# Moving half of a conversion to VectorE and counting four groups in a row, in a two-layer graph kernel

## The chip, the cores and the metric

The kernel runs on one core of a Trainium2 chip. The metric is the device time of one execution in microseconds (us); the median of three runs stands for a kernel. Before the change it is 272.93 us (272.83 to 273.19).

## The reference

Two graph layers over 4096 nodes with 64 features and a dense 4096x4096 adjacency of zeros and ones (about 16 ones in a row).

```python
# layer 0: each row weighs its last 100 neighbours by powers of 1/2, by rank within the row
support = x @ W0
rank = cumsum(adj != 0, axis=1); deg = rank[:, -1:]; k = minimum(deg, 100)
pos = rank - (deg - k)
w = mask * where(pos > 0, 0.5 ** (k - pos), 0)
x = layernorm(x + w @ support + b0)
# layer 1: mean over the neighbours, linear, relu, row norm
h = (adj @ x + x) / (sum(adj, 1) + 1)
out = relu(concat([x, h]) @ W1 + b1)
x = layernorm(x + out / maximum(norm(out), 1e-12))
```

## The kernel before

The transposed adjacency is cut into 8 **slabs** g of 512 target rows, and each slab into 8 **groups** k of 512 source rows, k running from 7 down to 0. A group (g, k) is a tile `a` of 128x4x512 in bf16, 512 KB in SBUF, cast from f32 by the DMA that loads it. Every group is loaded once. The 64 groups in the order (0,7), (0,6) ... (0,0), (1,7) ... (7,0) are numbered j = 0 to 63 here, and the main loop takes one group in each **step** i = 0 to 63, so step i works on group j = i, and slab g takes the steps 8g to 8g+7.

One step puts these pieces on TensorE, in this order: the **counts** of groups of the next chunk (`count`, line 233: how many ones each column has, four matmuls a group), **weigh** (line 261: eight half-size matmuls at line 270 and four at line 280, whose result in PSUM is the exponent of the weight; ScalarE turns one half of it into `w` at line 287, VectorE the other at line 288), up to four matmuls of the **second** layer (`some_sums`, line 344, matmul at line 307), **spread** (line 252, one matmul `rep`, and ScalarE's `near` at line 257), and **gather** of the step before (line 293, four matmuls at line 298). Then follow the hooks of the layer-0 epilogue: pz in step 8g+9, px in 8g+13, pu in 8g+14, and their parts on ScalarE, VectorE and GpSimd.

A **chunk** is a run of groups of one slab that share one `near`. Chunks are of one group in slab 0, two in slabs 1 to 3, four in slabs 4 to 7 (line 92). While a chunk is worked on, the groups of the next one are counted: `shares` (line 511) deals them out over its steps and joins two at a time, so that a chunk of two counts the two next groups in its first step, and a chunk of four counts two in its first and two in its third step. A chunk's count ends in an eviction `cs` by VectorE (line 247, or 249 for the first of a slab), which `spread` reads. TensorE, VectorE and ScalarE each run their instructions in this written order.

**Loads and buffers.** `load_next` (line 100) issues the loads on GpSimd's queue; six go out ahead of the loop, and step i issues load i+6. The bf16 tiles have 23 buffers (line 77). So load 23 and every later one needs a buffer that an earlier group has given back, and buffers are handed out in the order in which they come free. A group gives its buffer back in one of three ways:

- groups k = 7 to 4 of slabs 0 to 3 are copied to fp8 by `keep_next` (line 313), a half group (128x1024) in each of the steps 8 to 39, on ScalarE (line 320); the buffer is free after the second half;
- groups listed in `jobs` (line 325) give it back once the second layer has used them (line 307). The list is worked off in its order, one group a step, and a group k may be used from step 8(k+1)+6 on (`ready`, line 332), when x1hl, the layer-0 result of slab k, is there. Its first entries are (0,0), (0,1), (1,0), (1,1), (2,0), (2,1), (3,0), its last (6,0), (6,1), (6,2);
- the others stay to the end.

GpSimd's queue also carries the loads of x (`load_x`, step 8g+3) and the sums `add_b0` (step 8g+7). It runs in order: a load that waits for its buffer holds back everything behind it.

After step 63 the rest of the second layer runs, with the epilogue of layer 1.

Of the kernel before, what the change touches and what calls it, by code (L numbers as in the profile page):

```python
# [40 lines left out]
def adj_resnorm_kernel(  # L41
# [26 lines left out]
    nc = tc.nc  # L68
    D = w0.shape[0]
    NG, NK = adjT.shape[0], adjT.shape[1]  # L70
# [18 lines left out]

    chunks = []  # L90
    for g in range(NG):
        n = 1 if g == 0 else 2 if g < 4 else 4
        chunks += [[(g, k) for k in range(k0, k0 - n, -1)] for k0 in range(NK - 1, -1, -n)]
    steps = [s for c in chunks for s in c]
    when = {s: i for i, s in enumerate(steps)}

    A = [[None] * NK for _ in range(NG)]
    loads = iter(steps)

    def load_next(n=1, pieces=1):  # L100
        for _ in range(n):
            s = next(loads, None)
            if s is None:
                return
            g, k = s
            a = a16p.tile([P, KB, R], BF16, tag="a16", name=f"a16_{g}_{k}")
            for h in range(pieces):
                qs = slice(h * KB // pieces, (h + 1) * KB // pieces)
                nc.gpsimd.dma_start(out=a[:, qs, :], in_=adjT[g, k][:, qs, :])  # L109
            A[g][k] = a  # L110
# [8 lines left out]
    def load_xp(k):  # L119
        nc.gpsimd.dma_start(out=xp[:, ts(k, KB), :], in_=x_pairs[:, ts(k, KB), :])  # L120
# [112 lines left out]
    def count(g, k, first, last):  # L233
        if first:
            cnt[g] = ps_m.tile([P, R], F32, tag="m", name=f"cnt_{g}_{k}")
        for q in range(KB):
            nc.tensor.matmul(  # L237
                cnt[g][q * 32 : (q + 1) * 32, :],
                lhsT=pick[:, PW - 2 * k : PW - 2 * k + 32],
                rhs=A[g][k][:, q, :],  # L240
                start=first,
                stop=last,
            )
        if last:
            new = one.tile([P, R], BF16, tag="cs", name=f"cs_{g}_{k}")
            if g in cs:
                nc.vector.tensor_tensor(new, cnt[g], cs[g], ALU.add)  # L247
            else:
                nc.vector.tensor_copy(new, cnt[g])
            cs[g] = new  # L250

    def spread(g, k):

        pr = ps_m.tile([P, R], F32, tag="m", name=f"rep_{g}_{k}")
        nc.tensor.matmul(pr, lhsT=further, rhs=cs[g], start=True, stop=True)  # L255
        near[g] = epi.tile([P, R], BF16, tag="near", name=f"near_{g}_{k}")
        nc.scalar.activation(near[g], pr, AF.Relu, bias=most, scale=-1.0)  # L257
# [3 lines left out]
    def weigh(g, k, nr):  # L261

        w = wp.tile([P, KB, R], I16, tag="w", name=f"w_{g}_{k}")
        v = [ps_v.tile([P, 2, R], F32, tag="v", name=f"v_{g}_{k}_{i}") for i in range(2)]
        for i in range(2):
            for r in range(2):
                for c in range(2):
                    nc.tensor.matmul(  # L270
                        v[i][halves[c], r, :],
                        lhsT=tri[halves[r], :],
                        rhs=A[g][k][halves[r], 2 * i + c, :],
                        start=True,
                        stop=False,
                    )
        for i in range(2):
            for r in range(2):
                rows = slice((2 * i + r) * 32, (2 * i + r + 1) * 32)
                nc.tensor.matmul(  # L280
                    v[i][:, r, :],
                    lhsT=mine[rows, 2 * k : 2 * k + 2, :],
                    rhs=nr[rows, :],
                    start=False,
                    stop=True,
                )
        nc.scalar.activation(w[:, 0:2, :], v[0], AF.Relu, bias=less)  # L287
        nc.vector.tensor_scalar(w[:, 2:4, :], v[1], -STEP * MAX_NEIGH, 0.0, ALU.add, ALU.max)  # L288
        return w
# [3 lines left out]
    def gather(g, k, w):  # L293
        if k == NK - 1:
            acc0[g] = ps_a.tile([P, R], F32, tag="acc0", name=f"acc0_{g}")
        for q in range(KB):
            b = k * KB + q
            nc.tensor.matmul(  # L298
                acc0[g],
                lhsT=xhl[:, b, :],  # L300
                rhs=w[:, q, :].bitcast(BF16),
                start=(k, q) == (NK - 1, 0),
                stop=(k, q) == (0, KB - 1),
            )
# [5 lines left out]
    to_keep = [(g, k, h) for g in range(KEPT) for k in range(NK - 1, KEPT - 1, -1) for h in range(2)]  # L310
    kept = {}

    def keep_next():
        if not to_keep:
            return
        g, k, h = to_keep.pop(0)
        if h == 0:
            kept[g, k] = a8p.tile([P, KB, R], F8, tag="a8", name=f"a8_{g}_{k}")
        qs = slice(h * KB // 2, (h + 1) * KB // 2)
        nc.scalar.copy(kept[g, k][:, qs, :], A[g][k][:, qs, :], saturate=False)  # L320
        if h == 1:
            A[g][k] = kept[g, k]

# [7 lines left out]

    def ready(i, g, b):
        k = b // KB
        return i >= NK * (k + 1) + 6 and i >= when[g, k]

    def evict_part(g):
        acc = acc1.pop(g)
        if g in part:
            nc.vector.tensor_tensor(part[g], acc, part[g], ALU.add)
        else:  # L340
            part[g] = const.tile([P, R], F32, name=f"part_{g}")
            nc.vector.tensor_copy(part[g], acc)

    def some_sums(i, n):

        done = None
        while n and todo and done is None and ready(i, todo[0][0], todo[0][1]):
            g, b, first, last = todo.pop(0)
            if first:
                acc1[g] = ps_a.tile([P, R], F32, tag="acc1", name=f"acc_part_{g}_{b}")  # L350
            second(acc1[g], g, b, first, last)
            have[g] = b // KB + 1
            n -= 1
            if last:
                done = g
        return done
# [104 lines left out]
    def run(i, engine):  # L461
        for fn, args in hooks.pop((i, engine), []):
            fn(*args)

    for k in range(NK):
        i = when[0, k]
# [7 lines left out]
    for g in range(NG - 1):  # L474
        i = NK * (g + 1)
# [32 lines left out]
    for c, chunk in enumerate(chunks):  # L508
        ahead = chunks[c + 1] if c + 1 < len(chunks) else []
        n, m = len(chunk), len(ahead)  # L510
        shares = [ahead[i * m // n : (i + 1) * m // n] for i in range(n)]
        for i in range(0, n - 1, 2):

            shares[i : i + 2] = [shares[i] + shares[i + 1], []]
        nr = near[chunk[0][0]]
        for (g, k), share in zip(chunk, shares):
            i = when[g, k]
            run(i, ACT)
            run(i, POOL)
            load_next()  # L520
            if i < 3:
                load_xp(2 - i)

            w = weigh(g, k, nr) if i == 0 else None
            for s in share:
                count(*s, s == ahead[0], s == ahead[-1])
            w = w or weigh(g, k, nr)
            run(i, "ACT, late")
            done = some_sums(i, QUOTA)
            if share and share[-1] == ahead[-1]:  # L530
                spread(*ahead[-1])
            if i >= NK:
                keep_next()
            if held is not None:
                gather(*held)
            held = (g, k, w)
            run(i, PE)
            run(i, DVE)
            if done is not None:
                evict_part(done)  # L540
# [278 lines left out]
```

## Time and profile before

| | |
|---|---|
| median of 3 runs | 272.93 us |
| the profiled execution | 273.33 us |
| its span, first to last instruction | 271.5 us |
| TensorE busy in the span | 87% |
| VectorE, ScalarE, GpSimd busy | 65%, 58%, 23% |
| mean granted TensorE clock | 0.965 |
| loads of the adjacency | 65 DMAs, 9.7 us median to landing |
| conversions to fp8 on ScalarE | 32 of 1.04 us |
| counts evicted (`cs`), spreads (`rep`, `near`) | 28 each |

The profile comes from one execution. Its page shows busy shares by engine and by fortieth of the span; the timeline lists every instruction of an engine with its start, its length, and what ended the idle time before it; another answer gives the time from a DMA's issue to its landing. A matmul's length there is from start to modelled end, so matmuls in a row overlap: the distance from one start to the next is what a piece costs. Where a step's work begins is seen from its group of eight matmuls `v<-a,tri` of line 270: step 7 begins at 35.39 us, step 16 at 64.88, step 24 at 89.47, step 32 at 114.59, step 56 at 191.94.

### The profile page before, as it was taken

What the parts mean: (1) busy time and instruction counts of PE and PEld (TensorE: products, weight loads), DVE (VectorE), ACT (ScalarE), POOL (GpSimd) and SP (SyncE); (2) the same over time, 40 slices, a digit from 0 to 9 for tenths busy, and PEclk for the clock granted to TensorE, in tenths of its full rate; (3) what the DMA queues carried; (4) which work ended last, traced back from release to release, by engine and by line L of the source; (5) the groups of instructions that cost most, each with busy time, mean ns of one, the idle gap of its engine ahead of it and who ended that gap; (6) DMA issues with size and microseconds to landing.
All of it is one profiled execution on the core that took longest, in us unless ns stands there. A gap on an engine that the chain in (4) does not pass through costs nothing.

```text
span 271.5 us, 4838 instructions
## 1 busy us (share of the span) xinstructions
PE 237.3 (87%) x1865; PEld 105.0 (39%) x1865; DVE 176.3 (65%) x480; ACT 157.9 (58%) x226; POOL 61.9 (23%) x111
## 2 busy tenths in 40 slices
PE   8397688979899999999899999999998999997820
PEld 2122124334434343443344344434343546555710
DVE  5566634875596778367846684576577456597884
ACT  4456627897798869768854463436545322146351
POOL 8565551231101320322122121210200000221100
PEclk9979959999999999999999999999999999999985
DMA  6999999999997999799999999990500000010010
GB/s 97 195 230 234 241 212 214 222 214 214 223 214 141 165 211 214 124 171 214 182 179 205 203 162 180 168 168 12 98 2 0 0 2 0 0 42 20 19 58 21
DMA packets 12072, 37.13 MB, mean 137 GB/s; under 512 B 2066, under 2 KB 3218, under 8 KB 12050
## 3 DMA queue, kind: packets, MB, share of 16 engines
q0 software_dynamic: 10128, 35.66, 68.1%
q1 hardware_dynamic: 1922, 1.18, 1.5%
q8 instruction: 14, 0.23, 0.3%
q14 instruction: 8, 0.07, 0.1%
HBM read 69.34 MB, written 1.05 MB: 259 GB/s over the span
## 4 chain that ended last, share of the span: by engine, by line
PE 51%; DVE 11%; ACT 8%; issue 3%; POOL 1%; DVEq 0%; POOLq 0%; ACTq 0%
PE acc L298 10%; PE acc_part L307 9%; PE v L270 8%; PE v L280 5%; ACT w L287 4%; PE acc_right L307 3%; DVE w L288 3%; PE cnt L237 3%; PE vb L307 3%; PE pu L447 2%; PE va L307 2%; PE pz L594 2%; PE pz L395 2%; DVE x L422 1%; ACT a L320 1%
## 5 line engine op out<-in xcount | busy, mean ns | idle before, releaser
L288 DVE TENSOR_SCALAR w<-v 128x1024 int16<-128x1024 f32 x64 | 78.2, 1222 | 45.3 <-PE v L280 45.2
L287 ACT ACTIVATE w<-v,less 128x1024 int16<-128x1024 f32 x64 | 71.3, 1114 | 56.9 <-PE v L280 39.9
L298 PE MATMUL acc<-w,xhl 128*128 128x512 bf16 x256 | 67.2, 385 | 2.4 <-ACT hT L389 2.1
L109 POOL DMA_DIRECT2D a<-in_adjT_dram x65 | 35.5, 548 | 122.1 <-PE acc_part L307 49.9
L270 PE MATMUL v<-a,tri 64*64 64x512 bf16 x512 | 42.0, 397 | 4.3 <-ACT w L287 2.6
L298 PEld LDWEIGHTS <-xhl 128*128 128x128 f16 x256 | 23.9, 99 | 32.5 <-issue 9.5
L320 ACT CAST a<-a 128x1024 fp8e4<-128x1024 bf16 x32 | 33.3, 1039 | 0.0
L307 PEld LDWEIGHTS <-x1hl 128*128 128x128 f16 x224 | 19.8, 98 | 27.0 <-issue 5.7
L307 PE MATMUL acc_part<-a,x1hl 128*128 128x512 bf16 x108 | 28.0, 381 | 1.8 <-ACT x1hl L434 1.3
L247 DVE TENSOR_TENSOR cs<-cnt,cs 128x512 bf16<-128x512 f32 x20 | 13.8, 691 | 20.5 <-PE cnt L237 20.4
L237 PE MATMUL cnt<-a,pick 128*32 128x512 bf16 x256 | 21.9, 399 | 6.0 <-DMA a<-in_adjT_dram 6.0
L280 PE MATMUL v<-near,mine 32*128 32x512 bf16 x256 | 25.7, 391 | 0.2 <-ACT near L257 0.2
L270 PEld LDWEIGHTS <-tri 64*64 64x64 bf16 x512 | 12.6, 106 | 30.2 <-issue 28.0
L257 ACT ACTIVATE near<-rep,most 128x512 bf16<-128x512 f32 x28 | 19.1, 682 | 3.8 <-PE rep L255 3.7
L633 POOL TENSOR_TENSOR y<-y,x 128x256 f32<-128x256 f32 x7 | 5.0, 726 | 56.1 <-DVE y L630 56.1
L280 PEld LDWEIGHTS <-mine 32*128 32x128 bf16 x256 | 6.5, 91 | 24.9 <-issue 24.9
L255 PE MATMUL rep<-cs,further 128*128 128x512 bf16 x28 | 11.2, 400 | 3.7 <-DVE cs L247 1.7
L307 PE MATMUL acc_right<-a,x1hl 128*128 128x512 fp8e4 (+1 forms) x56 | 12.7, 379 | 0.0
L237 PEld LDWEIGHTS <-pick 128*32 128x32 bf16 x256 | 4.6, 94 | 19.8 <-issue 11.5
L655 ACT ACTIVATE o<-y,off,r_l 128x64 f32<-128x64 f32 x28 | 9.7, 428 | 3.1 <-issue 1.7
L382 DVE BATCH_NORM_STATS2 st_l<-y 128x6 f32<-128x64 f32 x60 | 9.0, 214 | 0.7 <-POOL y L633 0.6
L427 ACT CAST x1hl<-x 128x256 f16<-128x256 f32 x8 | 3.2, 406 | 10.1 <-DVE x L422 10.1
(139 smaller groups left out, 238.6 us busy)
## 6 DMA issues: line engine op xcount, KB each, us to landing
a<-in_adjT_dram POOLq DMA_DIRECT2D x63, 512.0 KB, 9.7
c<-in_x_pairs_dram POOLq DMA_DIRECT2D x8, 128.0 KB, 11.6
x<-in_x_dram POOLq DMA_DIRECT2D x8, 128.0 KB, 7.9
out_dram<-o SPq DMA_DIRECT2D x7, 128.0 KB, 1.7
a<-in_adjT_dram POOLq DMA_DIRECT2D x2, 256.0 KB, 4.7
out_dram<-o_7a SPq DMA_DIRECT2D x1, 64.0 KB, 1.9
out_dram<-o_7b SPq DMA_DIRECT2D x1, 64.0 KB, 1.5
w_sb<-in_L_gnn_weight_dram SPq DMA_DIRECT2D x2, 16.0 KB, 6.5
```

Source lines behind the costliest of these rows:

```text
L109: nc.gpsimd.dma_start(out=a[:, qs, :], in_=adjT[g, k][:, qs, :])
L237: nc.tensor.matmul(cnt[g][q * 32 : (q + 1) * 32, :], lhsT=pick[:, PW - 2 * k : PW - 2 * k + 32], rhs=A[g][k][:, q, :], start=first, stop=last,
L247: nc.vector.tensor_tensor(new, cnt[g], cs[g], ALU.add)
L255: nc.tensor.matmul(pr, lhsT=further, rhs=cs[g], start=True, stop=True)
L257: nc.scalar.activation(near[g], pr, AF.Relu, bias=most, scale=-1.0)
L270: nc.tensor.matmul(v[i][halves[c], r, :], lhsT=tri[halves[r], :], rhs=A[g][k][halves[r], 2 * i + c, :], start=True, stop=False,)
L280: nc.tensor.matmul(v[i][:, r, :], lhsT=mine[rows, 2 * k : 2 * k + 2, :], rhs=nr[rows, :], start=False, stop=True,)
L287: nc.scalar.activation(w[:, 0:2, :], v[0], AF.Relu, bias=less)
L288: nc.vector.tensor_scalar(w[:, 2:4, :], v[1], -STEP * MAX_NEIGH, 0.0, ALU.add, ALU.max)
L298: nc.tensor.matmul(acc0[g], lhsT=xhl[:, b, :], rhs=w[:, q, :].bitcast(BF16), start=(k, q) == (NK - 1, 0), stop=(k, q) == (0, KB - 1),)
L307: nc.tensor.matmul(acc, lhsT=x1hl[:, b, :], rhs=A[g][b // KB][:, b % KB, :], start=first, stop=last)
L320: nc.scalar.copy(kept[g, k][:, qs, :], A[g][k][:, qs, :], saturate=False)
```

## The change

Four edits.

1. **Chunks** (line 92): one group in slabs 0 and 1, two in slab 2, four in slabs 3 to 7.
2. **Shares**: where the next chunk has more than one group, all of it is counted in the first step of the present chunk. So a chunk of four counts its four next groups in a row in its first step.
3. **Conversion**: the half groups of the odd steps go to VectorE as a `tensor_copy` (the same 128x1024 from bf16 to fp8), those of the even steps stay on ScalarE. Each group so has one half on each engine, and its buffer is free after VectorE's.
4. **Loads and readiness**: the steps 16, 17 and 18 issue two loads each, so that step i from 18 on issues load i+9 in place of i+6; and the second layer may use a group from step 8(k+1)+7 on in place of +6.

```diff
     for g in range(NG):
-        n = 1 if g == 0 else 2 if g < 4 else 4
+        n = 1 if g < 2 else 2 if g < 3 else 4
         chunks += [[(g, k) for k in range(k0, k0 - n, -1)] for k0 in range(NK - 1, -1, -n)]
...
-    def keep_next():
+    def keep_next(i):
...
-        nc.scalar.copy(kept[g, k][:, qs, :], A[g][k][:, qs, :], saturate=False)
+        if i % 2:
+            nc.vector.tensor_copy(kept[g, k][:, qs, :], A[g][k][:, qs, :], saturate=False)
+        else:
+            nc.scalar.copy(kept[g, k][:, qs, :], A[g][k][:, qs, :], saturate=False)
...
     def ready(i, g, b):
         k = b // KB
-        return i >= NK * (k + 1) + 6 and i >= when[g, k]
+        return i >= NK * (k + 1) + 7 and i >= when[g, k]
...
         shares = [ahead[i * m // n : (i + 1) * m // n] for i in range(n)]
-        for i in range(0, n - 1, 2):
-            shares[i : i + 2] = [shares[i] + shares[i + 1], []]
+        if m > 1:
+            shares = [ahead] + [[]] * (n - 1)
...
-            load_next()
+            load_next(2 if 2 * NK <= i < 2 * NK + 3 else 1)
...
             if i >= NK:
-                keep_next()
+                keep_next(i)
```

## The prediction

> **What bounds the kernel now.** I read the page first: TensorE is busy 87% of the span, and the chain that ended last is mostly TensorE. Then the fortieths, where the loads show:
>
> ```profile
> PEclk9979959999999999999999999999999999999985
> DMA  6999999999997999799999999990500000010010
> ```
>
> The DMA engines are full until about 81 us (the 13th digit is the first 7 after the start) and the clock dips twice, the second time at 34 to 41 us. Then TensorE's timeline by steps. Steps 7, 24 and 55 to 56, each line a start, a length and the idle time before it:
>
> ```profile
> 34.84 0.62 PE L237 MATMUL cnt<-a,pick 128*32 128x512 bf16 x4 [2.68 <-DMA a<-in_adjT_dram]
> ...
> 89.47 0.63 PE L270 MATMUL v<-a,tri 64*64 64x512 bf16 x8
> 90.03 0.39 PE L280 MATMUL v<-near,mine 32*128 32x512 bf16 x4
> 90.35 1.04 PE L307 MATMUL acc_part<-a,x1hl 128*128 128x512 bf16 x4
> 91.22 0.38 PE L255 MATMUL rep<-cs,further 128*128 128x512 bf16 x1
> 91.44 1.03 PE L298 MATMUL acc<-w,xhl 128*128 128x512 bf16 x4
> ...
> 188.68 0.63 PE L270 MATMUL v<-a,tri 64*64 64x512 bf16 x8
> 189.24 0.39 PE L280 MATMUL v<-near,mine 32*128 32x512 bf16 x4
> 189.57 1.04 PE L307 MATMUL acc_part<-a,x1hl 128*128 128x512 bf16 x4
> 190.44 1.03 PE L298 MATMUL acc<-w,xhl 128*128 128x512 bf16 x4
> 191.40 0.62 PE L237 MATMUL cnt<-a,pick 128*32 128x512 bf16 x8
> 191.94 0.63 PE L270 MATMUL v<-a,tri 64*64 64x512 bf16 x8
> ```
>
> Step 24 has no gap: each piece starts where the one before ends. Start to start, weigh costs 0.56 + 0.33, second 0.87, rep 0.22, gather 0.96 (0.86 before a hook); elsewhere in the timeline a counted group costs 0.28, pz 1.01, px 0.53, pu 0.99. Until step 8 the loads bound the kernel (`cnt` waits seven times for them, 6.0 us in all, 2.68 the longest), from step 24 on TensorE's own work.
>
> Third, GpSimd's timeline, for loads that wait for a buffer:
>
> ```profile
> 83.19 0.53 POOL L109 DMA_DIRECT2D a<-in_adjT_dram  x1 [5.03 <-ACT a L320]
> 84.60 0.53 POOL L109 DMA_DIRECT2D a<-in_adjT_dram  x1 [0.88 <-PE rep L255]
> ...
> 190.90 0.53 POOL L109 DMA_DIRECT2D a<-in_adjT_dram  x1 [11.30 <-PE acc_part L307]
> ```
>
> These are loads 30, 31 and 63. Load 63 takes the buffer of (6,0), used last by the `acc_part` at 189.57. It is issued 2.22 us after its step's start and lands 5.0 later; so does load 30, issued into an idle queue. That is the least that any load after the first shows. With the queue full loads land 2.45 us apart: the times to landing of loads 13 to 27 put 13 at 44.6, 19 at 59.7, 23 at 69.6, 27 at 79.8.
>
> Last the clock, by stretches (length; TensorE, its loads, VectorE, ScalarE, GpSimd; clock; DMA share; GB/s):
>
> ```profile
> 24.00:28.00 4.00, 2.77 (x24) 0.91 (x23) 2.42 (x4) 2.40 (x4) 2.08 (x4) 1.00 1.06 242
> 30.60:34.00 3.40, 1.26 (x8) 0.31 (x7) 1.60 (x5) 1.86 (x3) 1.80 (x4) 1.00 1.07 224
> 34.00:40.80 6.80, 5.96 (x37) 1.40 (x36) 2.55 (x4) 1.69 (x2) 3.66 (x7) 0.50 1.06 213
> 40.80:44.20 3.40, 2.84 (x29) 1.03 (x22) 1.93 (x3) 2.61 (x4) 0.53 (x1) 1.00 1.07 214
> ```
>
> After 3.4 us at 37% busy the clock is halved for 6.8; stretches at 69% keep it.
>
> **What the Trainium skill says.** "TensorE: Matmul & The Clock Gate", Part 1: a free-running window of about 3.4 us, the clock halved after an idle one and restored after a busy one. The rows above agree: halved stretches of 3.4 (13.5 to 16.9) and 6.8 us. "VectorE: DVE Perf Modes", the perf-mode tier table: a copy in SBUF runs at four, two or one elements a cycle, by type and place; no such fp8 copy is in the trace. "SBUF: State Buffer", two separate sides: a VectorE copy in a two-port mode locks GpSimd out, which writes the load descriptors. The trace doesn't isolate it.
>
> **The change part by part.**
>
> *Conversion.* ScalarE loses 16 x 1.04 = 16.6 us. VectorE's price: row L214 turns 256 f32 into f16 in SBUF in 0.28 us; a four times larger copy at the same two a cycle is some 0.7 (estimate: 0.28 us + 768 elements two a cycle of the same page's 0.96 GHz, 0.40 us). Both ends, by the skill's modes: 0.4 and 1.2. So 16 x 0.7 = 11 us on an engine that is 65% busy, on odd steps, where it waits 2 us or more for TensorE in most (2.03 before `w` at 115.69). I take nothing; if the cover is gone, at 1.2, up to 0.5 a step in steps 13, 21, 29, 37.
>
> *Chunks.* Slab 1 spreads four times more and slab 3 twice less: two more `rep` (0.22), `cs` (0.69), `near` (0.68). In slab 1 the loads hide it.
>
> *Steps 7 to 22: gain, then lost to the loads.* Step 7 counts one group, not two, so the 2.68 us and the dip behind it go. Singles then follow the landings, and by adding pieces I get step 16 at about 60.1, against 64.88. But step 22 now counts loads 24 to 27 at once. Load 27 lands at 79.4 (79.8 less some 0.4, since the x load now stands behind it); the DMA has been full from the start, so nothing earlier in the kernel moves it. TensorE is there at about 75.5. Its weigh starts at 79.7 (before: 81.64): 1.9 us are left.
>
> *Step 24: a new wait.* It counts 28 to 31 in one go, at the head of the step. By the order of instructions load 31, group (3,0), takes the buffer of (0,1), which the second layer gives back in step 23, one step later than before. Step 23 starts at 79.7 + 0.56 + 0.33 + 0.22 + 0.86 + 0.99 = 82.7, load 31 is issued at +2.2 and lands at +5.0: 89.9; with the last 0.28 and some issue, step 24 starts at 90.3, against 89.47. Before, 31 was counted in step 30. Behind the waiting count stand all of TensorE's work, VectorE's `cs` and, after it, `w`. So the gain up to here is -1.9 + 2.7 = +0.8. The extra loads of steps 16 to 18 do nothing here: buffers and DMA decide.
>
> *Steps 24 to 55.* Work before: 31 steps x 1.85, less 12 x 0.1, hooks 10.1, 32 groups counted 8.8, 10 rep 2.2, 21 second 18.3: 95.6 of the 99.2 us, so 3.6 us of waits. After: 28 groups, 8 rep, 22 second (one was delayed): 94.8. Of the waits, 0.93 (rep on ScalarE's x1T at 109.26) and 0.52 (second on x1hl at 133.71) go with the new counts and readiness, 0.32 (on `part`) probably; I leave 1.9 for steps without second, where `w` sets the pace. 96.7, that is -2.5 (bounds -0.8 and -4.4). The other counts of four have their last load 0.1 to 3 us early by the same sum (steps 28, 32 and 40 under 0.5): nothing, at worst 1 each.
>
> *Step 56: the second new wait.* It counts 60 to 63, and load 63 still takes the buffer of (6,0), given back in step 55. So step 56 starts 2.22 + 5.0 + 0.4 = 7.6 after step 55, not 3.26: +4.35, and 0.55 less in step 58, which counted before. GpSimd's `add_b0` of slab 6 stands behind load 63, but is wanted only in step 58.
>
> Sum with the clock steady: +0.8 - 2.5 + 4.35 - 0.55 = +2.1.
>
> *The clock.* At step 24 TensorE idles some 3.8 us in two parts, at 56 some 3.7. A window of 3.4 us then lies mostly idle, as the one at 37%. The dips before cost half of what was left of them after the wait: 1.7 (13.5 to 16.9) and 3.0 (34.84 to 40.8). I take the mean, 2.35, at step 24 and the low end, 1.7, at 56, where the steps after 57 have no second and wait for `w`; nothing at step 22, where idle comes in short pieces (up to 1.5). +4.05.
>
> **Sum.** +6.15. Against the profiled execution, 273.33 (span 271.5 and 1.83 around it), 279.5; the median lies 0.4 lower: 272.93 + 6.1 = 279.0.
>
> **The rivals.**
> - *B, waits without dips.* The window falls so that neither is idle enough, or the later waits vanish wholly: +2.1, 275.0. For: the phase isn't fixed, and 64 to 69% busy kept the clock. Against: 3.7 us idle in any phase leaves a window about half idle.
> - *C, faster: the loads of slabs 1 to 3 land earlier.* If load 27 lands before 77.4, everything behind moves with it until TensorE is the bound (75.5): step 24 at 86.3, no dip at 24, and a short one at 56; -4 + 2.1 + 0 = -1.9, 271.0. It decides from a landing at 77.4 on. Against: 2.45 us held for fifteen loads whatever the engines did.
> - *D, more waits than two.* VectorE's copies lock GpSimd out just when loads follow them (35, 39, 47), and steps 28, 32, 40 wait up to 1 us each: +9, 282.0. For: margins under 0.5. Against: a copy is short and a dip delays the counts as well.
> - *That the counts don't wait*, because a load finds another buffer: excluded by the order of instructions, in which the last use of (0,1) and (6,0) stands just before these counts.
>
> **How the numbers follow.** A 0.62 (own range 276.5 to 281.5), B 0.17, D 0.11, C 0.07, and 0.03 near nothing. About 0.2% is what a measurement of this kernel tells from no change. Faster is C, 0.07; same 0.03; slower the rest, 0.90. From B's lower end to D: 274.2 to 282.5.
>
> **What would show it.** The `cnt` of step 24 waits for a DMA 2 us or more, and that of step 56 over 3; loads 31 and 63 land 5 us after their issue; the clock digit dips near 90 and near 195 us; no wait at 34.84; conversions on VectorE near 0.7. Wrong if step 24 starts before 87, or if TensorE doesn't wait at 56.

## The result, and the profile after

The changed kernel takes 285.77 us, the median of four runs (283.48 to 288.34), where the kernel before took 273.06 beside it (272.83 to 273.31). The run of 288.34 us counts as slow, because it lies more than 1.5% above the fastest, and the ratio of the means of the other runs is 1.044, with a 95% interval of 1.033 to 1.055. The forecast was 279.0 us with a range up to 282.5. The direction was right and the loss about twice as large as said: 12.7 us between the medians, not 6.1. The profiled execution of the changed kernel took 283.81 us, its span 281.9, so in the profile 10.4 us are to be found.

The page first: the clock, and then the chain that ended last, before (its clock stands in the prediction) and after.

```profile
PE 51%; DVE 11%; ACT 8%; issue 3%; POOL 1%; DVEq 0%; POOLq 0%; ACTq 0%
```

```profile
PEclk9659999999999799999999999999799999999985
...
PE 43%; DVE 12%; DMA 12%; ACT 4%; issue 3%; POOL 1%; ACTq 0%; DVEq 0%; POOLq 0%
```

The clock's dip at 34 to 41 us is gone; the new ones are at the 14th digit (92 to 99 us) and at the 29th (197 to 204 us). In the chain before, no DMA stood at all; now loads are 12% of it. Its steps that are DMAs, each with its start and its length:

```profile
85.34 5.42 DMA a<-in_adjT_dram
99.12 6.67 DMA a<-in_adjT_dram
112.52 7.46 DMA a<-in_adjT_dram
125.50 8.49 DMA a<-in_adjT_dram
196.21 4.97 DMA a<-in_adjT_dram
```

These are loads 31, 35, 39, 43 and 63: each is the last load of a count of four. TensorE's timeline shows what they hold up. The first row is the count in step 8, which waits for load 9; the others are the fourth group counted (with the idle time before it) in steps 24, 28, 32, 36 and 56, and the start of weigh behind two of them:

```profile
34.92 0.40 PE L237 MATMUL cnt<-a,pick 128*32 128x512 bf16 x4 [0.61 <-DMA a<-in_adjT_dram]
...
90.81 0.40 PE L237 MATMUL cnt<-a,pick 128*32 128x512 bf16 x4 [3.17 <-DMA a<-in_adjT_dram]
91.14 0.67 PE L270 MATMUL v<-a,tri 64*64 64x512 bf16 x8
...
105.84 0.40 PE L237 MATMUL cnt<-a,pick 128*32 128x512 bf16 x4 [0.29 <-DMA a<-in_adjT_dram]
...
120.02 0.40 PE L237 MATMUL cnt<-a,pick 128*32 128x512 bf16 x4 [2.09 <-DMA a<-in_adjT_dram]
...
134.03 0.40 PE L237 MATMUL cnt<-a,pick 128*32 128x512 bf16 x4 [1.72 <-DMA a<-in_adjT_dram]
...
201.22 0.62 PE L237 MATMUL cnt<-a,pick 128*32 128x512 bf16 x4 [3.69 <-DMA a<-in_adjT_dram]
201.77 1.07 PE L270 MATMUL v<-a,tri 64*64 64x512 bf16 x8
```

Step 24 also waits 0.79 us for its third group. Load 9, for which step 7 waited 2.68 us before, is now counted a step later, in step 8, and the wait for it is down to 0.61 us. Read as starts of steps, before against after:

| | before | after | difference grows by |
|---|---|---|---|
| step 16 | 64.88 | 62.29 | -2.6 |
| step 22 | 81.64 | 79.85 | +0.8 |
| step 24 | 89.47 | 91.14 | +3.5 |
| step 32 | 114.59 | 120.35 | +4.1 |
| step 40 | 139.91 | 146.26 | +0.6 |
| step 48 | 167.02 | 172.62 | -0.8 |
| step 56 | 191.94 | 201.77 | +4.2 |
| end of the span | 271.5 | 281.9 | +0.6 |

The conversion on VectorE is among the groups of the page, and one copy costs what was estimated (0.7 us):

```profile
L322 DVE CAST a<-a 128x1024 fp8e4<-128x1024 bf16 x16 | 10.9, 684 | 0.0
```

### The profile page after: what moved, and what is told of

Its sections match the earlier page's. It is cut to its first block, busy times and chain, and to the rows that moved or that the text cites. A ratio compares the mean times of both kernels' runs of the same rounds, so it can differ in the third digit from the quotient of the medians.

```text
span 281.9 us, 4828 instructions
## 1 busy us (share of the span) xinstructions
PE 236.0 (84%) x1836; PEld 106.1 (38%) x1867; DVE 187.2 (66%) x498; ACT 144.8 (51%) x212; POOL 64.0 (23%) x111
## 4 chain that ended last, share of the span: by engine, by line
PE 43%; DVE 12%; DMA 12%; ACT 4%; issue 3%; POOL 1%; ACTq 0%; DVEq 0%; POOLq 0%
DMA a<-in_adjT_dram 12%; PE acc L298 8%; PE acc_part L307 7%; PE v L270 7%; PE v L280 4%; DVE w L288 4%; PE acc_right L307 3%; PE vb L307 2%; PE cnt L237 2%; ACT w L287 2%; PE va L307 2%; PE pu L451 2%; PE pz L598 2%; PE pz L399 2%; DVE x L426 1%
## 5 line engine op out<-in xcount | busy, mean ns | idle before, releaser
L298 PE MATMUL acc<-w,xhl 128*128 128x512 bf16 x240 | 64.0, 384 | 3.3 <-ACT hT L393 1.5
L109 POOL DMA_DIRECT2D a<-in_adjT_dram x65 | 37.8, 583 | 125.8 <-PE acc_part L307 57.1
L247 DVE TENSOR_TENSOR cs<-cnt,cs 128x512 bf16<-128x512 f32 x22 | 15.2, 690 | 22.3 <-PE cnt L237 22.3
L307 PE MATMUL acc_part<-a,x1hl 128*128 128x512 bf16 x96 | 26.6, 396 | 1.9 <-issue 1.9
L257 ACT ACTIVATE near<-rep,most 128x512 bf16<-128x512 f32 x30 | 20.5, 683 | 6.0 <-PE rep L255 5.8
L270 PEld LDWEIGHTS <-tri 64*64 64x64 bf16 x512 | 11.5, 106 | 24.3 <-issue 22.9
L237 PEld LDWEIGHTS <-pick 128*32 128x32 bf16 x256 | 6.3, 95 | 32.7 <-issue 23.7
L324 ACT CAST a<-a 128x1024 fp8e4<-128x1024 bf16 x16 | 16.6, 1040 | 0.0
L307 PE MATMUL acc_right<-a,x1hl 128*128 128x512 fp8e4 (+1 forms) x55 | 12.7, 379 | 0.1
L322 DVE CAST a<-a 128x1024 fp8e4<-128x1024 bf16 x16 | 10.9, 684 | 0.0
L249 DVE CAST cs<-cnt 128x512 bf16<-128x512 f32 x8 | 5.5, 691 | 6.2 <-PE cnt L237 6.2
```

Of the source, the lines that this page charges most:

```text
L237: nc.tensor.matmul(cnt[g][q * 32 : (q + 1) * 32, :], lhsT=pick[:, PW - 2 * k : PW - 2 * k + 32], rhs=A[g][k][:, q, :], start=first, stop=last,
L270: nc.tensor.matmul(v[i][halves[c], r, :], lhsT=tri[halves[r], :], rhs=A[g][k][halves[r], 2 * i + c, :], start=True, stop=False,)
L298: nc.tensor.matmul(acc0[g], lhsT=xhl[:, b, :], rhs=w[:, q, :].bitcast(BF16), start=(k, q) == (NK - 1, 0), stop=(k, q) == (0, KB - 1),)
L307: nc.tensor.matmul(acc, lhsT=x1hl[:, b, :], rhs=A[g][b // KB][:, b % KB, :], start=first, stop=last)
```

## The experiments

All are timed beside the kernel before, which stayed at 273.1 to 273.3 us (medians). "After" is the changed kernel, 285.77 us. Starts of steps are from the timelines of the profiled runs.

**1. The counts dealt two and two, as before the change.** Everything else stays changed.

```diff
-        if m > 1:
-            shares = [ahead] + [[]] * (n - 1)
+        for i in range(0, n - 1, 2):
+            shares[i : i + 2] = [shares[i] + shares[i + 1], []]
```

> The changed kernel with its counts dealt out as before: two groups in the first and two in the third step of a chunk of four. Theory W (the time goes into counts of four that ask for their last load two steps early): the waits of the count for a DMA at steps 24, 28, 32, 36 and 56, 11.7 us in the profile, go, and with them the halved clock behind two of them, some 2.7 us; 285.8 falls to 270 to 273. Rival V (VectorE's conversions hold up w and, by the shared port, GpSimd's loads): the conversions are all still there, so it stays within 2 us of 285.

Measured: 269.53 us (269.2 to 269.58), a ratio of 0.987 (0.985 to 0.988). No count waits for a load after 40 us, and the clock shows no dip between 20 us and the tail. So the whole loss lies in the counts of four in the first step of a chunk, 16.2 us between the medians and 14.2 between the two profiles, and the rest of the change gains 3.6 us.

**2. Readiness one step earlier (+6), as before the change; counts of four kept.**

```diff
-        return i >= NK * (k + 1) + 7 and i >= when[g, k]
+        return i >= NK * (k + 1) + 6 and i >= when[g, k]
```

> The changed kernel with the second layer allowed from step 8(k+1)+6 on again. Theory W with load 31 behind (0,1): the buffer of (0,1) comes free one step earlier, so the wait at step 24 (3.96 us) shrinks by about a step, to 0.5 to 1.5; the wait at 56 stays (the use of (6,0) is in step 55 either way); 280 to 283. Rival V: no change, 284 to 288. Rival R (the later readiness alone is the loss, since it holds back all buffers by a step): waits at 24, 32 and 36 all but gone and 277 or less.

Measured: 281.61 us (281.45 to 282.13). The wait at step 24 falls to 2.18 us, those at 32 and 36 to 0.2 or less, the one at 56 stays at 3.92. The time lies in W's window, the wait at step 24 does not (W had 0.5 to 1.5): load 31 is issued 2.7 us sooner, but takes 7.3 us to land. Buffers that come back one step sooner take some 4 us off the median (2 off the profiled run) and leave the larger part. That the readiness alone is the cause is refuted.

**3. Only the conversion: the kernel before with the half groups of odd steps on VectorE.**

```diff
+        if i % 2:
+            nc.vector.tensor_copy(kept[g, k][:, qs, :], A[g][k][:, qs, :], saturate=False)
+        else:
```

> The kernel before with nothing but the conversion of the odd steps on VectorE. Theory W: hidden, 271 to 274, no new wait of a count for a DMA. Rival V: 276 or more, with w of VectorE later and loads landing later than in the kernel before.

Measured: 271.82 us (271.74 to 271.9), 0.995 (0.994 to 0.997). In the kernel before, then, the conversion gains 1.3 us and shows no loss. One count that did not wait there, at 40.06 us, now waits 0.83 us for a load, against W's "no new wait", but step 8 begins at 40.39 against 40.34. The wait at step 7 stays as it was:

```profile
35.09 0.40 PE L237 MATMUL cnt<-a,pick 128*32 128x512 bf16 x4 [2.68 <-DMA a<-in_adjT_dram]
```

**4. The changed kernel with all conversions on ScalarE.**

```diff
-        if i % 2:
+        if False:
```

> The changed kernel with every half group converted on ScalarE again. Theory W: no gain, 285 to 290, since the counts of four wait as before, and buffers given back by conversions come no sooner from ScalarE's longer queue. Rival V: most of the loss goes, 273 to 279.

Measured: 283.74 us (282.2 to 284.09), 1.3 us under W's window and level with the profiled run of the changed kernel. The waits at steps 24 and 56 stay (0.67 + 2.99 and 3.79 us), so these two don't come from VectorE's copies. For steps 28 to 36 this run doesn't settle it: only step 32 still waits, 0.92 us, where the three wait 4.1 us in the changed kernel. Loads 39 and 43 land 6.1 us after their issue here, not 7.5 and 8.5; but with the copies left in place they land after 6.9 and 5.5 us in experiment 7. Rival D of the prediction blamed the copies for waits at steps 28, 32 and 40. They came at 28, 32 and 36; that the copies caused them isn't shown.

What a copy does to a load can be read from GpSimd's issues. The first row is load 34 in the changed kernel, issued just before a copy on VectorE that runs from 97.90 to 98.58 us, the second the same load in this experiment:

```profile
97.87 0.82 POOL L109 DMA_DIRECT2D a<-in_adjT_dram  x1 [2.87 <-PE acc_part L307]
99.04 0.53 POOL L109 DMA_DIRECT2D a<-in_adjT_dram  x1 [3.45 <-PE acc_part L307]
```

From 50 us on eight issues of the changed kernel meet a copy. They take 0.79 to 0.83 us and each ends 0.12 us after its copy; all others, and all in this experiment, take 0.57 or less. Loads 31 and 34 land 5.42 and 5.47 us after such an issue begins, 5.13 and 5.12 us where no copy meets it. So a copy does hold up the issue of a load, which the trace before could not show, and it costs that load 0.3 us.

**5. Only the counts at steps 24 and 56 dealt two and two.**

```diff
             shares = [ahead] + [[]] * (n - 1)
+            if ahead[-1] in ((3, 0), (7, 0)):
+                shares = [ahead[:2], [], ahead[2:], []]
```

> The changed kernel, except that the two counts of four that end in group (3,0), at step 24, and in group (7,0), at step 56, are dealt two and two over their chunk. W (a count of four waits because its last load can be issued only one step before it; each wait is local): the waits of 3.96 and 3.69 us and both clock dips go (about 2.9), those at steps 28 to 36 stay or grow by up to 2: 273.5 to 277 us. V (the loads of slabs 3 to 7 are late as a whole, and a wait that is taken away at step 24 comes back in full at the next count of four): 279 or more.

Measured: 272.69 us (271.37 to 278.57 in twenty runs), 0.8 us under W's window. The two waits and the dips behind them are gone. TensorE's timeline shows which waits are left, at steps 28 and 32, and the chain's DMAs are loads 35 and 39:

```profile
101.21 0.40 PE L237 MATMUL cnt<-a,pick 128*32 128x512 bf16 x4 [1.48 <-DMA a<-in_adjT_dram]
...
115.20 0.40 PE L237 MATMUL cnt<-a,pick 128*32 128x512 bf16 x4 [1.90 <-DMA a<-in_adjT_dram]
```

```profile
92.54 8.63 DMA a<-in_adjT_dram
107.89 7.27 DMA a<-in_adjT_dram
```

Without any stall at step 24 these two loads still need 8.6 and 7.3 us. So their lateness is their own, and not an echo of the stall. Behind the wait of step 32 the clock is halved once more, from 116.54 to 119.95 us. Against the first experiment the remaining fours cost 3.2 us, this dip included.

**6. The complement: fours only at steps 24 and 56, all counts from step 28 on dealt two and two.**

```diff
             shares = [ahead] + [[]] * (n - 1)
+            if m == 4 and ahead[-1] not in ((3, 0), (7, 0)):
+                shares = [ahead[:2], [], ahead[2:], []] if n == 4 else [ahead, []]
```

> The other half of the split at steps 24 and 56 alone: the changed kernel, where those two counts stay four in a row and all other counts of four from step 28 on are dealt two and two. W (the prediction's own case: waits only at these two steps, and the missing part of its sum lies in the waits at steps 28 to 36): 278.5 to 281 us, waits of 3.5 to 4.5 us in all at each of the two steps, none of a count between 95 and 190 us, and the repeats within 1.5 us. V (the two big waits are worth all of the loss, the others overlap with them): 283 us or more.

Measured: 281.5 us (281.12 to 282.14), half a microsecond over W's window, and no count waits between 95 and 190 us. This comes close to the kernel that the prediction in fact computed, with waits at these two steps and nowhere else. Its step 24 starts at 91.07 us, step 55 at 190.54 and step 56 at 198.59. From the start of step 24 to that of step 55, which the prediction calls steps 24 to 55, it takes 99.47 us, where the prediction had 99.05 with its dip and the changed kernel has 102.85. Load 63 is issued 2.22 us into step 55 and lands 5.23 us later, as the chain shows:

```profile
85.22 5.49 DMA a<-in_adjT_dram
192.76 5.23 DMA a<-in_adjT_dram
```

Against the first experiment the two big waits and their dips cost 12.0 us, and 3.2 + 12.0 = 15.2 us, of the 14.2 (profiles) to 16.2 (medians) between the first experiment and the changed kernel.

**7. The clock: twelve matmuls of zeros between the third and the fourth group of the counts at steps 24 and 56.** They add zero to the count.

```diff
                 count(*s, s == ahead[0], s == ahead[-1])
+                if s in ((3, 1), (7, 1)):
+                    for _ in range(12):
+                        nc.tensor.matmul(cnt[s[0]], lhsT=none, rhs=A[g][k][:, 0, :], start=False, stop=False)
```

> The changed kernel with 12 matmuls of zeros (2.6 us of TensorE at full clock) put between the third and the fourth group of the two counts at steps 24 and 56, where TensorE would only wait; they add zero to the same counts. D (the idle of these waits halves the clock behind them, 1.3 to 1.6 us each): both clock dips go, the waits shrink by what the fillers take, steps 25 and 57 start 1.3 to 1.6 earlier: 280.5 to 282.5 us, and the repeats lie within 1 us of each other. N (the dips cost nothing by themselves, because loads set the pace behind them): 283 to 286, as the changed kernel.

Measured: 279.07 us (278.36 to 282.7); three of the four runs lie within 0.9 us of each other, as D expected, the fourth 3.5 above them, and D's window was missed by 1.4 us, on the low side. The windows show that the dips go. Each row is a stretch, its length, and the busy time of TensorE, its loads, VectorE, ScalarE and GpSimd, then the clock. First the changed kernel:

```profile
88.40:91.80 3.40, 0.99 (x16) 0.31 (x15) 0.55 (x1) 0.00 (x0) 0.00 (x0) 0.97 1.07 210
91.80:95.20 3.40, 3.40 (x13) 1.13 (x13) 2.13 (x4) 1.68 (x2) 0.53 (x1) 0.53 0.27 54
197.50:200.90 3.40, 0.04 (x4) 0.00 (x0) 0.00 (x0) 0.00 (x0) 0.51 (x2) 0.99 0.86 181
200.90:204.30 3.40, 3.08 (x19) 0.82 (x19) 1.46 (x2) 0.83 (x1) 0.71 (x1) 0.51 0.01 5
```

Then the kernel with the fillers:

```profile
88.40:91.80 3.40, 2.88 (x22) 1.09 (x20) 0.36 (x1) 0.00 (x0) 0.00 (x0) 1.00 1.05 212
91.80:95.20 3.40, 3.40 (x30) 1.21 (x27) 2.31 (x4) 2.82 (x4) 0.53 (x1) 1.00 0.48 72
193.60:197.00 3.40, 2.63 (x12) 1.06 (x11) 0.00 (x0) 0.00 (x0) 0.40 (x1) 1.00 0.85 180
197.00:200.40 3.40, 2.94 (x24) 1.14 (x24) 2.20 (x3) 1.55 (x2) 0.72 (x1) 1.00 0.02 8
```

A stretch of 3.4 us that is mostly idle is followed by one at half clock; with the fillers neither is there. The Trainium skill, "TensorE: Matmul & The Clock Gate", Part 1, describes a free-running window of about 3.4 us and a halved clock after an idle one. The rows agree, and show that a window need not be wholly idle: after 29% and 1% busy the clock was 0.53 and 0.51, after 85% and 77% it stayed at 1.00. Step 24 to 25 takes 2.93 us in place of 4.51, and step 56 to 57 2.93 in place of 4.02: the dips cost 1.6 and 1.1 us in that profile. In the sixth experiment the second cost 2.6 (step 56 to 57 took 5.49, less 2.93).

How busy a window must be can be worked out here. In every profile of this case, from the first change of the clock to the last, the stretches at full and at half clock are multiples of 3.41 us, so their edges fix the windows. Cut at these edges from the first change on, the profiles of the two kernels and of the twelve variants have 1071 windows. A window at full clock is followed by one at half clock where TensorE is busy 44% of it or less, and never where it is busy 51% or more. A window at half clock is followed by one at full clock where TensorE is busy 88% or more, and never at 85% or less. Between these figures no window lies. Three windows of the sixth experiment, around step 56, and two of the fifth, around step 32:

```profile
194.03:197.44 3.41, 0.06 (x4) 0.00 (x0) 0.00 (x0) 0.00 (x0) 0.53 (x2) 1.00 0.89 173
197.44:200.86 3.42, 2.82 (x18) 0.68 (x18) 1.20 (x2) 0.58 (x1) 0.71 (x1) 0.50 0.04 16
200.86:204.27 3.41, 3.41 (x12) 1.09 (x14) 1.47 (x3) 1.31 (x3) 0.00 (x0) 0.50 0.00 0
...
113.13:116.54 3.41, 1.51 (x21) 0.46 (x17) 0.69 (x1) 0.00 (x0) 0.53 (x1) 1.00 0.90 150
116.54:119.95 3.41, 3.41 (x9) 1.03 (x7) 1.98 (x3) 2.39 (x3) 0.53 (x1) 0.50 0.99 174
```

So the price of a wait depends on where it falls. Behind step 56 the halved window of the changed kernel is 88% busy and the clock comes back; in the sixth experiment it is 83% busy and a second halved window follows, hence 1.1 and 2.6 us. The wait of 1.90 us in the fifth experiment lies in one window and halves the clock. That of 2.09 us at step 32 of the changed kernel is split over two, which stay 70% and 67% busy, and the clock stays full.

The rest of the gain in the seventh experiment's profile (5.1 us of span in all) was not foreseen: with step 24 shortened, load 43 is issued 2.15 us sooner and lands in 5.5 us, not 8.5, and the wait at step 36 is gone.

**8. Fours in a row, one step later, and two steps later.** Nothing is dealt out; the block of four counts moves from the first step of the chunk to the second, then to the third.

```diff
             shares = [ahead] + [[]] * (n - 1)
+            if n == 4:
+                shares = [[], ahead, [], []]      # one step later
+                shares = [[], [], ahead, []]      # two steps later
```

> The changed kernel, except that every count of four stands in the second step of its chunk in place of the first; still four groups in a row. W (what costs is that the count comes too early for its last load, not that four are counted in a row): the waits at steps 24 to 36 go, of the one at step 56 about 1.0 of 3.69 us stays, both dips go or are short: 269.5 to 273 us. V (four in a row cost by themselves, since the weighing behind them and with it w come late): 276 or more.

> The changed kernel, except that every count of four stands in the third step of its chunk; still four groups in a row. W (only the earliness costs; a load of the later half of a chunk needs two to three steps from its issue to its count): no DMA wait of a count after 40 us, no clock dip after 20 us, 269.0 to 270.2 us, and repeats within 0.5 us. V (four in a row have a price of their own, which the version one step later at 271.1 hides among its last waits): 270.6 us or more, without a DMA wait of a count.

Measured: one step later 271.09 us (270.86 to 271.44), inside W's window, with waits of 1.41, 0.21 and 1.08 us left near steps 25, 29 and 57. Two steps later 268.2 us (267.9 to 268.25), a ratio of 0.981 (0.979 to 0.982): no count waits after 40 us. That is the fastest version of all, and 0.8 us under W's window. So counting four in a row has no price by itself; in the third step it even beats two and two by 1.3 us, which wasn't followed further. The page of this last version, clock and chain:

```profile
PEclk9869999999999999999999999999999999999975
...
PE 54%; DVE 12%; ACT 5%; issue 2%; POOL 1%; ACTq 0%; DVEq 0%; POOLq 0%
```

No dip between the start and the tail, no DMA in the chain, and TensorE carries more of it than in either kernel.

**9. Where the rest of the change gains.** Three variants of the first experiment: single loads in steps 16 to 18; slab 3 by twos; readiness +6.

```diff
-            load_next(2 if 2 * NK <= i < 2 * NK + 3 else 1)
+            load_next()                                       # first variant
-        n = 1 if g < 2 else 2 if g < 3 else 4
+        n = 1 if g < 2 else 2 if g < 4 else 4                 # second variant
-        return i >= NK * (k + 1) + 7 and i >= when[g, k]
+        return i >= NK * (k + 1) + 6 and i >= when[g, k]      # third variant
```

> The changed kernel with the counts dealt two and two (269.5 us) and with one load a step throughout. W (the extra loads of steps 16 to 18 do nothing, since buffers and a full DMA queue decide when a load starts): 269.2 to 269.9 us. X (they bring later loads forward, which the counts of slab 3 need): 270.3 us or more, with a DMA wait of a count between 80 and 110 us.

> The changed kernel with the counts dealt two and two (269.5 us), and slab 3 counted by twos as before the change. W (larger chunks in slab 3 spare two spreads, each with a matmul of 0.22 us and a wait for it): 269.6 to 270.5 us. V (what that version gains over the conversion alone, 271.8, comes from slab 3): 271.3 or more.

> The changed kernel with the counts dealt two and two (269.5 us), and the second layer's sums ready one step earlier, as before the change (6 in place of 7). W (buffers come back a step earlier, but nothing waits for a load there any more): 269.2 to 270.3 us, with short waits of the sums on x1hl, as the kernel before has. V (earlier loads still help): 268.8 or less.

Measured: 269.45 (269.28 to 269.53), 269.78 (269.55 to 269.86) and 270.48 us (270.38 to 270.74). Against 269.53 the extra loads give nothing, the larger chunks of slab 3 some 0.2 us, which the repeats hardly tell from nothing, and the later readiness 0.9, which W had put at 0.8 at most. With the conversion's 1.3 that leaves, by subtraction, 1.1 to 1.2 us of the 3.6 for the singles of slab 1, which weren't run alone; at step 22 the first experiment is 1.1 us ahead of the third (80.04 against 81.17 us).

## Why the prediction was off

**The start: right.** Step 7's wait of 2.68 us and the dip behind it went.

**Step 22: right in the number, in part by luck.** It was put at 79.7 us by the landing of load 27, at 79.4. Load 27 landed at 79.48 and step 22 came at 79.85. But the sum had TensorE ready at 75.5 us and waiting for the load. It came to this count only at 78.65. The first three groups start 0.22 us apart and the fourth, at 79.52, 0.43 after the third, so the wait for the load was 0.2 us, where the sum had almost 4. The gain was spent earlier. "In slab 1 the loads hide it", it was said of the additional spreads; in fact TensorE waits 3.2 us there for `near` and `cs` (0.64, 1.17 and 1.38 us, between 44 and 54 us), and step 16 came at 62.29 us, not at 60.1. The two limits happened to meet at step 22.

**Step 24: right in kind, 0.8 us short.** It was put at 90.3 us and came at 91.14. One half is that step 23 began 0.4 us later than in the sum, the other that load 31 took 5.42 us rather than 5.0, with an issue that a copy on VectorE held up by 0.3.

**Step 56: right.** 7.6 us after step 55 by the sum, 7.78 measured; load 63 took 4.97 us.

**The clock: right in kind.** Both dips came where they were put; they cost 1.6 and 1.1 us in the profile, against 2.35 and 1.7 assumed, and 2.6 for the second one in experiment 6. Rival B, waits without dips, is out: in every profile in which TensorE idled for 3.6 us or more at one of these steps, a dip followed.

**The conversion: right** in price (0.684 us), and right in that it costs next to nothing: it gained 1.3 us in the kernel before, which wasn't counted, and held up single loads by 0.3 us, which was put at nothing.

**Steps 24 to 55: here the sum failed**, at the sentence "The other counts of four have their last load 0.1 to 3 us early by the same sum (steps 28, 32 and 40 under 0.5): nothing, at worst 1 each". The sum priced every landing at 5.0 us, the shortest that the profile of before has. Load 30, one of its two examples, was not issued into an idle queue, as the prediction has it: load 29 was still on its way and landed 1.5 us later. The last loads of steps 28, 32 and 36 took 6.67, 7.46 and 8.49 us, and the counts waited 0.29, 2.09 and 1.72, 4.1 us in all; 102.85 us for these steps in place of 99.05. With 5.0, load 39 would have landed at 117.5, 0.4 us before its count came to it (at 117.93). The profile of before had the warning: 9.7 us as the median of all its loads, and 6.7 to 10.8 for loads 31 to 46.

Experiment 6 takes out these waits: 99.47 us for the steps, 3.4 less than in the changed kernel, and 281.5 us in all. So of the 6.8 us between forecast and median, 4.3 are this term by the medians (285.77 less 281.5), a figure that the spread of the changed kernel blurs. The other 2.5 are left with these waits taken out: in experiment 6 step 24 is 0.8 us late (91.07 against 90.3), steps 24 to 55 take 0.4 more (the first dip costs 0.7 less, the work some 1.1 more), the way to step 56 0.4 more (8.05 against 7.6), and the second dip costs 2.6 in place of 1.7: 2.5 together.

What made these loads late is known for the first alone. Load 35 lands 2.46 us behind load 34, the spacing of a full queue. Loads 39 and 43 land 1.9 and 1.3 us later than the prediction's two figures (5.0 us from the issue, 2.45 behind the load in front) allow. An estimate from these figures, carried from load 34 on through the issue times of the profile, has load 39 at 117.5 and load 43 at 130.5 us, both before their counts (117.93 and 132.31). So pricing the queue would have foreseen 0.3 of the 4.1 us.

In the profiled execution of the changed kernel the same account closes: 0.8 at step 24, 3.8 in steps 24 to 55 (4.1 of waits and 0.4 of work, less 0.7 at the dip), 0.2 at step 56 and some -0.6 for the second dip make +4.2, and 6.15 + 4.2 is the measured 10.4.

**What stays open.** It is not shown why load 39 landed 4.4 us behind the load in front of it, with the DMA moving 131 GB/s from 116 to 120 us, where 2.45 us is the spacing of a full queue; whether VectorE's copies have a part in it is open too (experiment 4). The repeats of the changed kernel, the highest left out, lie up to 4.2 us apart. Experiments 2 and 6, which wait at steps 24 and 56 almost alone, spread by 0.7 and 1.0, and those without such a wait (1, 8 at its third step, and all of 9) by 0.4 or less, in four or five runs each. The kernel before, which has no such wait either, spreads by 1.4 us in 23 runs, so these short series say little. Landing times that vary, and a clock that is halved for one window or for two, are both possible sources; no run varied one of them alone.

## What to carry to other kernels

A consumer that takes several transfers at once waits for the last of them. Don't price that one at the landing of a lone load: take the landings that the profile shows near it, of which 5.0 us was the shortest and 9.7 the median here, and count the steps from its issue to its use. A block that comes too early is best moved later as a whole, not taken apart: two steps made the difference between 285.8 and 268.2 us here. A wait that leaves TensorE idle for a few microseconds can cost again after it ends, through the clock, and matmuls of zeros in the gap show how much.

## What had not been expected of the hardware

Loads of 512 KB to SBUF, cast from f32 on the way, took between 5.0 and 10.2 us from issue to landing in the changed kernel between 80 and 150 us. Load 39 took 7.5 us though the load in front of it landed only 3.1 us after its issue. In the profile of experiment 7, where a stall before it was 1.6 us shorter, load 43 landed in 5.5 us and not in 8.5. So a margin of a microsecond or two in front of such a load is no margin.

A copy of 0.68 us on VectorE held up a load's issue on GpSimd by 0.3 us (experiment 4). And the clock's windows of 3.41 us had a sharp limit: 44% busy halved the clock, 51% kept it, and once halved it took 88% to bring it back (experiment 7).
